# Two-layer graph network kernel: wider batches for gathering by rows, and a mask loaded for two groups at once

## The chip, the cores and the metric

The kernel runs on one core of one Trainium2 chip. Its metric is the device time of one execution in microseconds (us), lower being better. The median of three runs of the kernel before is 3950.51 us (3949.45 to 3950.6).

The engines are called PE (matrix products), DVE (vector), ACT (activations), POOL (GpSimd) and SP (Sync). SP, ACT and POOL each have a queue from which DMAs are issued, in the order of the program.

## The reference

The network has 12500 nodes with 128 features and 200000 edges that are sorted by destination. With `h = relu(layernorm(x))`:

```python
deg  = segment_sum(ones, dst, N);  wsum = segment_sum(edge_weight, dst, N)
w    = edge_weight / maximum(wsum, EPS)[dst]
feat = relu(h @ W_pool + b_pool)
neigh = segment_max(feat[src] * w[:, None], dst, N)          # layer 1
neigh = where(deg > 0, neigh, 0)
rst  = h @ W1_self + neigh @ W1_neigh + b1
h1   = relu(rst / maximum(norm(rst, axis=1), EPS))
neigh2 = segment_sum(h1[src] * w[:, None], dst, N) / maximum(deg, 1)   # layer 2
out  = x + relu(h1 @ W2_self + neigh2 @ W2_neigh + b2)
```

## The kernel before

**Stages.** A preparation normalises x, computes `feat` and writes it to `feat_d` in memory. Layer 1 then takes the edges in 391 groups of 512 (the last has 320), and writes its node results to `h_d`. Layer 2 takes the same 391 groups over `h_d` and writes the output. Each layer is one Python loop over "turns" `i`, which emits the instructions of several groups at different stages of their way (L638 for layer 1, L730 for layer 2). Each engine's instructions keep the order in which they are emitted.

**Gathers.** A group needs the source rows of its 512 edges: four chunks of 128 rows of 512 bytes. `gather` (L519) has POOL issue one indirect DMA for each chunk into the tile `gt` (L525), of which there are eight (L87), so that POOL can be at most eight groups ahead of the reader of `gt`.

**Chunks by rows.** In some groups chunk 0 does not come from POOL. The class `Rows` (L459) brings it into a tile `ga` by 128 DMAs of one row each, issued from SP's and ACT's queues. For group g, `load` (L494) has SP fetch the 128 source indices into a row `ri`, `shift` (L499) has DVE turn them into byte offsets, and `rows` (L502) loads a batch of offsets into registers of the issuing engine (a TENSOR_LOAD, L510) and issues one DMA for each (L514). The constructor's arguments say how often a group is taken (`every`) and how its rows are shared out: a list of (engine, rows, rows in a batch). `plan` spreads the batches of one chunk over the `every` turns that begin at turn g - every - 1. Before, layer 1 takes every 12th group (32 chunks), with 96 rows from SP in twelve batches of 8 and 32 rows from ACT in eight batches of 4 (L637). Layer 2 takes every 8th (48 chunks), with 64 rows from each queue in eight batches of 8 (L729). Groups 387 to 390 are never taken.

**A turn of layer 1.** SP issues its row batch (L640), stores a finished node tile if there is one (L576) and loads the mask `kt` of group i + 4 (L643). `kt` (L622 to L625) holds for each edge of a group whether its destination is that of the edge before, broadcast to all 128 partitions; seven tiles stand ready for it. POOL gathers group i. ACT scales the four chunks of group i by the edge weights (L654), waiting for the gathers and, in a taken group, for all rows of `ga`. PE transposes them into the tile `pm` (L655), of which there are two. DVE runs a segmented maximum over group i - 1 with `kt` (L661) and picks the results with two more operations (L669, L670), PE transposes these (L698) and puts them at their nodes' places (L710), and ACT writes the places of group i - 5 to `agg` (L703). Every fourth turn a tile of 128 nodes begins its own products (L552, L553). ACT's row batch stands at the turn's end (L713). Every second turn, some of the work on the edges' weights for later use goes to DVE as well.

**A turn of layer 2.** SP and ACT issue their row batches, POOL gathers group i, DVE builds a selection matrix of 192 columns, PE multiplies group i - 1 (L759) and DVE adds the sums of group i - 2 to `agg` (L764). A node tile's input is loaded and its output stored by SP every fourth turn (L585, L597).

**Semaphores of the DMAs.** In the built program, all DMAs of SP's and ACT's queues share eight semaphores, handed out in turn over both queues. A DMA waits until the one before it on its semaphore has landed. The order in which they are handed out is fixed when the program is built. In layer 1 it runs over turns that lie apart: SP's batch of a turn stands behind ACT's batches of turns some two to five later. POOL's gathers have eight semaphores of their own.

Of the kernel before, what the change touches and what calls it, by code (L numbers as in the profile page):

```python
# [8 lines left out]
BF16 = mybir.dt.bfloat16  # L9
# [9 lines left out]
P = 128  # L19
D = 128  # L20
G = 512
# [14 lines left out]
def gnn_kernel(ctx, tc, x, src, dst, ew, w_pool, b_pool, w1s, w1n, b1, w2s, w2n, b2, out):  # L36
# [13 lines left out]
    nc = tc.nc  # L50
# [6 lines left out]
    NG = GF + 1  # L57
# [7 lines left out]
    feat_d = dram.tile([NP, D], F32, name="feat_d")  # L65
    h_d = dram.tile([NP, D], F32, name="h_d")
    keep_d = dram.tile([NT * P, G], BF16, name="keep_d")
# [21 lines left out]
    wk = prep.enter_context(tc.tile_pool(name="n0", bufs=2))  # L89
# [293 lines left out]
    for i in range(len(groups) + 3):  # L383
        at = [groups[i - k] if 0 <= i - k < len(groups) else None for k in range(4)]
        if at[3]:
            t0, n = at[3]
# [7 lines left out]
        if at[2]:  # L394
            t0, n = at[2]
# [4 lines left out]
        if at[1]:  # L400
            t0, n = at[1]
# [11 lines left out]
        if at[0]:  # L413
            t0, n = at[0]
# [22 lines left out]
    def background():  # L437

        for t in range(1, NT):
            yield P * t - 4, edges1, t  # L440
        for t in range(NT):
            yield NG, edges2, t
        for t in reversed(range(NT)):
            yield NG, edges3, t
        for t in range(NT):
            yield NG, fitness, t
        yield NG, lambda get, t: verdict(get), 0

    def edges_of(g):

        ne = G if g < GF else TAIL
        return *divmod(g, P), ne, [(j, min(P, ne - j * P)) for j in range(-(-ne // P))]

    def pairs_of(g):

        t, r, ne, _ = edges_of(g)
        return t, r, ne, [(j, min(P, ne // 2 - j * P)) for j in range(-(-ne // (2 * P)))]
# [61 lines left out]
    def gather(pool, table_d, g, byrow=None):  # L519
        t, r, ne, chunks = edges_of(g)  # L520
        gt = pool.tile([P, Q, D], F32, name="gt")
        for j, k in chunks:
            if j == 0 and byrow and byrow.takes(g):
                continue
            nc.gpsimd.indirect_dma_start(  # L525
                out=gt[:k, j, :], out_offset=None, in_=table_d[:, :],
                in_offset=bass.IndirectOffsetOnAxis(ap=srcT[:k, t, j, r:r + 1], axis=0))
        return gt

    def turns(behind):  # L530

        out = {}
        g = i = 0
        for n in range(HI):
            while g < NG - 1 and (g + 1 - LAG) * RHO < (n + 1) * P:
                g += 1
            i = max(i + 1, g + behind)
            out[i] = n
        return out
# [64 lines left out]
    with tc.manual_schedule(), tc.tile_pool(name="ew", bufs=3) as wk, \  # L604
            tc.tile_pool(name="ep", bufs=2, space=PSUM) as ps:
        AHEAD = 4
        jobs = [(due, job(lambda: ps.tile([P, Q, P], F32, name="pq", bufs=1), t)) for due, job, t in background()]

        def side_step():

            while jobs:
                due, steps = jobs[0]
                if next(steps, jobs) is jobs:
                    jobs.pop(0)
                elif i < due:
                    break

        gts, kts, pms, scs, sels, prs, rws, pas = ({} for _ in range(8))
        turn = turns(6)
        busy = {}  # L620

        def keep_rows(g):  # L622
            ne = edges_of(g)[2]
            kts[g] = wk.tile([P, G], BF16, name="kt", bufs=AHEAD + 3)
            nc.sync.dma_start(kts[g][:, :ne], keep_d[g:g + 1, :ne].to_broadcast([P, ne]))  # L625

        def node_stage(k):
            if (i, k) in busy:
                st = busy.pop((i, k))
                next(st, None)  # L630
                if k < 5:
                    busy[i + 1, k + 1] = st

        for g in range(AHEAD):
            keep_rows(g)
        carry = NEG
        byrow = Rows(wk, feat_d, 12, [(nc.sync, 96, 8), (nc.scalar, 32, 4)])  # L637
        for i in range(max(turn) + 6):  # L638
            byrow.turn(i)
            byrow.rows(i, nc.sync)  # L640
            node_stage(5)
            if i + AHEAD < NG:
                keep_rows(i + AHEAD)  # L643
            if i < NG:
                gts[i] = gather(gp, feat_d, i, byrow)

            if i < NG:
                t, r, ne, chunks = edges_of(i)
                gs = wk.tile([P, Q, D], F32, name="gs", bufs=2)
                pms[i] = ps.tile([P, G], F32, name="pm")  # L650
                gt = gts.pop(i)
                for j, k in chunks:
                    rows_j = byrow.tile(i) if j == 0 and byrow.takes(i) else gt[:k, j, :]
                    nc.scalar.activation(gs[:k, j, :], rows_j, AF.Copy, scale=ewT[:k, t, j, r:r + 1])  # L654
                    nc.tensor.transpose(pms[i][:, j * P:j * P + k], gs[:k, j, :], ident[:k, :k])  # L655

            g = i - 1
            if 0 <= g < NG:
                ne = edges_of(g)[2]
                kt, pm = kts.pop(g), pms.pop(g)  # L660
                nc.vector.tensor_tensor_scan(pm[:, :ne], kt[:, :ne], pm[:, :ne], carry,  # L661
                                             op0=OP.add, op1=OP.max)
                if g + 1 < NG:
                    carry = wk.tile([P, 1], F32, name="carry")
                    nc.vector.tensor_copy(carry, pm[:, ne - 1:ne])
                sc = scs[g] = wk.tile([P, G // 2], F32, name="sc")
                two = pm[:, :ne].rearrange("p (c two) -> p c two", two=2)
                new = kt[:, :ne].bitcast(I16).rearrange("p (c two) -> p c two", two=2)
                nc.vector.tensor_copy(sc[:, :ne // 2], two[:, :, 1])  # L669
                nc.vector.copy_predicated(sc[:, :ne // 2], new[:, :, 1], two[:, :, 0])  # L670
            node_stage(1)
            node_stage(3)
            g = i - 3
            if 0 <= g < NG:
                t, r, ne, chunks = pairs_of(g)
                sels[g] = wk.tile([P, Q // 2, LW], F32, name="sel")
                for j, k in chunks:
                    nc.vector.tensor_scalar(  # L678
                        sels[g][:k, j, :], cols[:k, 1, :], lastT[:k, t, j, r:r + 1],
                        invT[:k, t, j, r:r + 1], op0=OP.is_equal, op1=OP.mult)  # L680

                rws[g] = wk.tile([P, Q // 2, D], F32, name="rows")
                pr = prs.pop(g)
                for j, k in (((slice(0, Q // 2), P),) if ne == G else chunks):
                    nc.scalar.activation(rws[g][:k, j, :], pr[:k, j, :], AF.Copy)  # L685

            node_stage(4)
            if i in turn:
                n = turn[i]
                st = nodes1(wk, ps, n, agg[:, n * P:(n + 1) * P])  # L690
                next(st)
                busy[i + 1, 1] = st
            g = i - 2
            if 0 <= g < NG:
                prs[g] = ps.tile([P, Q // 2, D], F32, name="pr")
                sc = scs.pop(g)
                for j, k in pairs_of(g)[3]:
                    nc.tensor.transpose(prs[g][:k, j, :], sc[:, j * P:j * P + k], ident)  # L698

            g = i - 5  # L700
            if 0 <= g < NG:
                at = window_at(mybir.EngineType.Activation, g)
                nc.scalar.activation(agg[:, bass.ds(at, LW)], pas.pop(g), AF.Copy)  # L703
            g = i - 4
            if 0 <= g < NG:
                chunks = pairs_of(g)[3]
                pas[g] = ps.tile([P, LW], F32, name="pa", bufs=1)
                rows, sel = rws.pop(g), sels.pop(g)
                for j, k in chunks:
                    nc.tensor.matmul(pas[g], rows[:k, j, :], sel[:k, j, :], start=j == 0,  # L710
                                     stop=j == len(chunks) - 1)
            node_stage(2)
            byrow.rows(i, nc.scalar)  # L713
            if i % 2:
                side_step()
        assert not busy
        i = NG
        side_step()


    with tc.manual_schedule(), tc.tile_pool(name="ew2", bufs=3) as wk, \
# [4 lines left out]
        gts, ss, pas, xrs = ({} for _ in range(4))  # L726
        turn = turns(3)
        late = None
        byrow = Rows(wk, h_d, 8, [(nc.sync, 64, 8), (nc.scalar, 64, 8)])  # L729
        for i in range(max(turn) + 2):  # L730
            byrow.turn(i)
            byrow.rows(i, nc.sync)
# [1 line left out]
            if i < NG:  # L734
                gts[i] = gather(gp, h_d, i, byrow)
                t, r, ne, chunks = edges_of(i)
# [11 lines left out]
            if i in turn:  # L748
                n = turn[i]
                late = nodes2(wk, ps, n, agg[:, n * P:(n + 1) * P], xrs.pop(n))  # L750
                next(late)
            g = i - 1
# [8 lines left out]
            g = i - 2  # L761
# [21 lines left out]
    with tc.If(flag > 0):  # L783
        with tc.tile_pool(name="gt", bufs=1) as tp, tc.tile_pool(name="gw", bufs=2) as wk, \
# [11 lines left out]
            for t0, n in node_groups():  # L796
                c = slice(t0 * P, (t0 + n) * P)
                k = n * P
# [87 lines left out]
```

## Time and profile before

| what | value |
|---|---|
| median of three runs | 3950.51 us |
| the profiled execution | 3949.8 us, of which its span 3947.9 us |
| POOL busy | 2946.2 us (75% of the span), 3105 instructions |
| PE busy | 2163.9 us (55%) |
| DVE busy | 1664.7 us (42%) |
| ACT busy | 795.0 us (20%) |
| first and last gather of layer 1 begin | 91.9 and 2023.9 us |
| first and last gather of layer 2 begin | 2045.8 and 3936.5 us |
| gathers of layer 1 and layer 2 | 1531 and 1515 |
| row DMAs of layer 1, SP and ACT | 3072 and 1024 |
| row DMAs of layer 2, SP and ACT | 3072 and 3072 |
| mask loads `kt` | 391, of 128 KB each (the last 80 KB) |

The page of a profile gives each engine's busy time, its groups of instructions (line, engine, operation, output and inputs, count, then busy time and mean, then the idle time just ahead of them and what ended most of it), and the waits. DMA-issuing instructions of SP and ACT are not counted as busy, and a DMA's arrival is not part of the issuing instruction's time. The indirect DMAs of POOL are counted[...].

### The profile page before, as it was taken

To read this page: it belongs to the slowest core of one execution; us is meant where nothing else is said; L and a number is where in the kernel's file an instruction comes from. 1 tells how busy PE (TensorE), PEld (TensorE's weight loads), DVE (VectorE), ACT (ScalarE), POOL (GpSimd) and SP (SyncE) were. 2 spreads that over 40 slices of the span, in tenths; PEclk is the share of its full clock that TensorE was granted. 3 is DMA by queue.
4 is the path that set the end of the run, shared out by engine and by line. 5 is a ranking of instruction groups with operands and counts; after the bars stand their busy time and mean duration, and the time that the engine had idled before them with its cause. 6 is when DMAs were issued, how large, how long until landed. Compare 5 with 4: busy or idle time off the path is not lost.

```text
span 3947.9 us, 55088 instructions
## 1 busy us (share of the span) xinstructions
PE 2163.9 (55%) x8349; PEld 1764.2 (45%) x8349; DVE 1664.7 (42%) x4700; ACT 795.0 (20%) x2907; POOL 2946.2 (75%) x3105
## 2 busy tenths in 40 slices
PE   6546546546555455445555555555555555555555
PEld 4335445435444344344444444444444444444444
DVE  7556656657656656556552222121221222222221
ACT  6334334334334334334320000000000000000000
POOL 5777777777777777777757777777777777777776
PEclk8555555555555555555555555555555555555555
DMA  6233333333333333333322222222222222222222
GB/s 170 75 83 85 84 84 84 84 83 82 84 84 82 85 85 84 85 86 83 86 65 61 62 63 61 62 62 62 62 62 62 62 62 62 62 62 62 62 62 58
DMA packets 245792, 295.43 MB, mean 75 GB/s; under 512 B 71023, under 2 KB 195518, under 8 KB 245424
## 3 DMA queue, kind: packets, MB, share of 16 engines
q0 software_dynamic: 97472, 199.75, 18.8%
q1 hardware_dynamic: 139024, 89.04, 8.4%
q10 hardware_dynamic: 8928, 3.03, 0.3%
q14 instruction: 296, 2.42, 0.2%
q8 instruction: 72, 1.18, 0.1%
HBM read 271.77 MB, written 19.77 MB: 74 GB/s over the span
## 4 chain that ended last, share of the span: by engine, by line
DMA 24%; POOL 23%; issue 17%; SPq 10%; PE 9%; DVE 7%; ACT 5%; ACTq 4%; POOLq 0%; DVEq 0%
POOL gt L525 23%; DMA gt<-h_d,srcT 14%; SPq L514 6%; PE pm L655 4%; DMA kt<-keep_d 4%; DVE pm L661 4%; DMA ga<-feat_d 3%; ACTq L514 3%; ACT gs L654 3%; SPq L510 2%; DMA ri<-in_src 1%; DMA gt<-feat_d,srcT 1%; PE pa L710 1%; SPq L625 1%; PE pn L552 1%
## 5 line engine op out<-in xcount | busy, mean ns | idle before, releaser
L525 POOL DMA_INDIRECT gt<-feat_d,srcT x1531 | 1466.1, 958 | 469.5 <-issue 391.4
L525 POOL DMA_INDIRECT gt<-h_d,srcT x1515 | 1429.5, 944 | 483.1 <-issue 388.3
L759 PE MATMUL pa<-s,gt 128*128 128x48 f32 x3030 | 967.9, 423 | 826.6 <-DMA gt<-h_d,srcT 736.1
L759 PEld LDWEIGHTS pa<-s,gt 128*128 128x128 f32 x3030 | 757.5, 312 | 1038.6 <-DMA gt<-h_d,srcT 818.6
L655 PE MATMUL pm<-ident,gs 128*128 128x128 f32 x1563 | 484.0, 439 | 902.0 <-DVE sc L670 497.3
L655 PEld LDWEIGHTS pm<-ident,gs 128*128 128x128 f32 x1563 | 288.5, 199 | 1038.2 <-issue 483.4
L764 DVE TENSOR_TENSOR agg<-pa,agg 128x48 f32 x391 | 81.2, 208 | 1439.3 <-PE pa L759 1025.7
L661 DVE TENSOR_TENSOR_SCAN pm<-kt,carry,pm 128x512 f32<-128x512 bf16 x390 | 499.3, 1280 | 255.1 <-DMA kt<-keep_d 118.2
L654 ACT ACTIVATE gs<-gt,ewT 128x128 f32<-128x128 f32 x1531 | 503.6, 392 | 357.0 <-DMA ga<-feat_d 200.6
L710 PEld LDWEIGHTS pa<-sel,rows 128*128 128x128 f32 x1564 | 352.5, 311 | 35.9 <-ACT agg L703 34.0
L710 PE MATMUL pa<-sel,rows 128*128 128x48 f32 x1564 | 358.0, 375 | 2.6 <-ACT agg L703 1.1
L698 PE MATMUL pr<-ident,sc 128*128 128x128 f32 x782 | 236.3, 403 | 0.8 <-DVE sc L670 0.7
L500 DVE TENSOR_SCALAR ri<-ri 1x128 int32<-1x128 int32 x80 | 18.2, 227 | 505.1 <-DMA ri<-in_src 495.7
L678 DVE TENSOR_SCALAR sel<-cols,lastT,invT 128x48 f32<-128x48 f32 x782 | 213.0, 327 | 0.0
L670 DVE COPY_PREDICATED sc<-kt,pm 128x256 f32<-128x256 int16 x391 | 173.0, 443 | 13.3
L698 PEld LDWEIGHTS pr<-ident,sc 128*128 128x128 f32 x782 | 163.0, 218 | 1.2 <-PE pa L710 1.0
L669 DVE COPY sc<-pm 128x256 f32<-128x256 f32 x391 | 162.0, 414 | 0.0
L741 DVE TENSOR_TENSOR s<-hit,w2T 128x192 f32<-128x192 f32 x391 | 139.8, 357 | 13.5
L685 ACT ACTIVATE rows<-pr 128x256 f32<-128x256 f32 x392 | 142.3, 363 | 2.2 <-PE pr L698 2.2
L739 DVE TENSOR_TENSOR hit<-iota,locT 128x192 f32<-128x192 f32 x391 | 139.1, 356 | 0.8
L703 ACT ACTIVATE agg<-pa 128x48 f32 x391 | 78.5, 201 | 162.4 <-PE pn L553 157.0
L565 ACT ACTIVATE sq<-r 128x128 f32<-128x128 f32 x98 | 29.7, 303 | 375.7 <-DVE r L561 375.7
(144 smaller groups left out, 1374.0 us busy)
## 6 DMA issues: line engine op xcount, KB each, us to landing
kt<-keep_d SPq DMA_DIRECT2D x390, 128.0 KB
ga<-feat_d SPq DMA_DIRECT2D x3072, 0.5 KB
ga<-h_d SPq DMA_DIRECT2D x3072, 0.5 KB
ga<-h_d ACTq DMA_DIRECT2D x3072, 0.5 KB
gt<-feat_d,srcT POOLq DMA_INDIRECT x1531
gt<-h_d,srcT POOLq DMA_INDIRECT x1515
ga<-feat_d ACTq DMA_DIRECT2D x1024, 0.5 KB
h_d<-h SPq DMA_DIRECT2D x98, 64.0 KB
```

What stands on the lines that cost most here:

```text
L514: eng.dma_start(ga[r + k:r + k + 1, :], self.bytes[None, bass.ds(at[k], 4 * D)])
L525: nc.gpsimd.indirect_dma_start(out=gt[:k, j, :], out_offset=None, in_=table_d[:, :], in_offset=bass.IndirectOffsetOnAxis(ap=srcT[:k, t, j, ...
L654: nc.scalar.activation(gs[:k, j, :], rows_j, AF.Copy, scale=ewT[:k, t, j, r:r + 1])
L655: nc.tensor.transpose(pms[i][:, j * P:j * P + k], gs[:k, j, :], ident[:k, :k])
L661: nc.vector.tensor_tensor_scan(pm[:, :ne], kt[:, :ne], pm[:, :ne], carry, op0=OP.add, op1=OP.max)
L669: nc.vector.tensor_copy(sc[:, :ne // 2], two[:, :, 1])
L670: nc.vector.copy_predicated(sc[:, :ne // 2], new[:, :, 1], two[:, :, 0])
L678: nc.vector.tensor_scalar(sels[g][:k, j, :], cols[:k, 1, :], lastT[:k, t, j, r:r + 1], invT[:k, t, j, r:r + 1], op0=OP.is_equal, op1=OP.mult)
L685: nc.scalar.activation(rws[g][:k, j, :], pr[:k, j, :], AF.Copy)
L698: nc.tensor.transpose(prs[g][:k, j, :], sc[:, j * P:j * P + k], ident)
L710: nc.tensor.matmul(pas[g], rows[:k, j, :], sel[:k, j, :], start=j == 0, stop=j == len(chunks) - 1)
L759: nc.tensor.matmul(pas[g], rows_j, s[:k, j, :], start=j == 0, stop=j == len(chunks) - 1)
```

## The change

Three things change. First, SP's batches of rows in layer 1 and both queues' batches in layer 2 become sixteen rows; ACT's in layer 1 stay at four. Second, layer 1 takes every 10th group instead of every 12th (38 chunks instead of 32), and layer 2 every 7th instead of every 8th (55 instead of 48). So 6 and 7 gathers go, and 13 times 128 row DMAs come. Third, `kt` is loaded for two groups at once, in odd turns: turn i loads groups i + 3 and i + 4. The number of its tiles falls from seven, of one group each, to the pool's own number, three (L604), of two groups each.

```diff
         def keep_rows(g):
-            ne = edges_of(g)[2]
-            kts[g] = wk.tile([P, G], BF16, name="kt", bufs=AHEAD + 3)
-            nc.sync.dma_start(kts[g][:, :ne], keep_d[g:g + 1, :ne].to_broadcast([P, ne]))
+
+            n = min(2, NG - g)
+            kt = wk.tile([P, 2, G], BF16, name="kt")
+            rows = keep_d[g:g + n, :]
+            nc.sync.dma_start(kt[:, :n, :], bass.AP(tensor=rows.tensor, offset=rows.offset,
+                                                    ap=[[0, P], [G, n], [1, G]]))
+            for k in range(n):
+                kts[g + k] = kt[:, k, :]
...
-        for g in range(AHEAD):
+        for g in range(0, AHEAD, 2):
             keep_rows(g)
         carry = NEG
-        byrow = Rows(wk, feat_d, 12, [(nc.sync, 96, 8), (nc.scalar, 32, 4)])
+        byrow = Rows(wk, feat_d, 10, [(nc.sync, 96, 16), (nc.scalar, 32, 4)])
         for i in range(max(turn) + 6):
             byrow.turn(i)
             byrow.rows(i, nc.sync)
             node_stage(5)
-            if i + AHEAD < NG:
-                keep_rows(i + AHEAD)
+            if i % 2 and i + AHEAD - 1 < NG:
+                keep_rows(i + AHEAD - 1)
...
-        byrow = Rows(wk, h_d, 8, [(nc.sync, 64, 8), (nc.scalar, 64, 8)])
+        byrow = Rows(wk, h_d, 7, [(nc.sync, 64, 16), (nc.scalar, 64, 16)])
```

The lines of `Rows`, `gather` and the loops are otherwise the same; from L626 on, the lines of layer 1 and layer 2 are numbered five higher.

## The prediction

> **What bounds the kernel now.** I read the groups of the page first, then POOL's timeline, then who waits on SP, DVE and ACT. In the groups, the last columns are busy time, mean ns, and the idle time ahead with what ended most of it:
>
> ```profile
> L525 POOL DMA_INDIRECT gt<-feat_d,srcT x1531 | 1466.1, 958 | 469.5 <-issue 391.4
> L525 POOL DMA_INDIRECT gt<-h_d,srcT x1515 | 1429.5, 944 | 483.1 <-issue 388.3
> ...
> L661 DVE TENSOR_TENSOR_SCAN pm<-kt,carry,pm 128x512 f32<-128x512 bf16 x390 | 499.3, 1280 | 255.1 <-DMA kt<-keep_d 118.2
> L654 ACT ACTIVATE gs<-gt,ewT 128x128 f32<-128x128 f32 x1531 | 503.6, 392 | 357.0 <-DMA ga<-feat_d 200.6
> ```
>
> POOL's timeline, far into layer 1 (start, duration, and in brackets the idle time before):
>
> ```profile
> 1600.41 0.94 POOL L525 DMA_INDIRECT gt<-feat_d,srcT  x1 [0.30 <-issue]
> 1601.66 0.95 POOL L525 DMA_INDIRECT gt<-feat_d,srcT  x1 [0.30 <-issue]
> 1602.91 0.95 POOL L525 DMA_INDIRECT gt<-feat_d,srcT  x1 [0.30 <-issue]
> ```
>
> A gather begins every 1.249 us, 0.945 of it busy and 0.305 between two. That holds throughout: layer 2's gathers begin from 2045.8 to 3936.5 us, 1890.7 us for 1514 steps, 1.2488 each. Layer 1's take 1932.0 us for 1530 steps, 1.2627; the trace puts the surplus of 21 us into 51 gathers of over 1.0 us, all before 1390 us, beside DVE's background work. POOL waits for no other engine, so it is the bound of both layers: a gather less is 1.2488 us less, as long as nothing else becomes late.
>
> What could become late is the chain by rows. SP's and DVE's longest waits in these stages, then the first use of the last chunk by rows in layer 1 beside POOL:
>
> ```profile
> SPq L514 <- DMA ga<-h_d: 301.4, 398, 5.4
> SPq L514 <- DMA ga<-feat_d: 257.8, 285, 5.4
> ```
>
> ```profile
> DVE ri L500 <- DMA ri<-in_src: 495.7, 35, 17.2
> DVE pm L661 <- DMA kt<-keep_d: 118.2, 64, 7.5
> ```
>
> ```profile
> 2012.62 0.94 POOL L525 DMA_INDIRECT gt<-feat_d,srcT  x1 [0.30 <-issue]
> 2012.80 0.40 ACT L654 ACTIVATE gs<-ga,ewT 128x128 f32<-128x128 f32 x1 [16.12 <-DMA ga<-feat_d]
> ```
>
> ACT starts group 384 at 2012.8 while POOL, counted back from its last gather, is at the second chunk of group 388. It would stop only at the start of group 392, where `gt` has no free tile, 15 gathers or 18.7 us on. In all 32 taken groups this lag (ACT's start less the end of the group's gathers) is 14 to 19 us, and ACT needs 8 to 11 turns to catch up. So layer 1's row chain is late in every cycle, and POOL is shielded from it by some 19 us.
>
> **What the Trainium skill says.** "Perfetto Trace Analysis", What "DMA-bound" means: an issuing queue whose track is solid DMA slices is bound by descriptor generation, not by data. POOL agrees (0.945 busy of 1.249). "DMA: Bandwidth & Descriptors", Anatomy of one DMA: about 2.0 us fixed plus bytes at 436 GB/s; the trace's gathers land 2.47 us and its `kt` loads of 128 KB 3.0 us after their issue begins. I take the difference for 128 KB more from it, an estimate of 0.3 us. The same page, Latency and other measured facts: a tensor_load takes about 600 ns at least. The trace shows 485 ns for most of ACT's loads of four registers, so the floor doesn't hold here; 742 ns is SP's median for eight:
>
> ```profile
> L510 SPq TENSOR_LOAD <-ri x768: 691/742/1054, 97.4 to 3884.8; - x192
> L510 ACTq TENSOR_LOAD <-ri x640: 312/823/1098, 98.9 to 3877.8; - x160
> ```
>
> **The change part by part.** *Gathers removed.* Multiples of 10 from 10 to 380 are 38, of 7 from 7 to 385 are 55, against 32 and 48. Layer 1 loses 6 x 1.2488 = 7.5 us, layer 2 7 x 1.2488 = 8.7 us: 16.2 us, if POOL stays fed.
>
> *Rows, layer 1, SP.* Its timeline where nothing waits:
>
> ```profile
> 1878.92 2.52 SPq L514 DMA_DIRECT2D ga<-feat_d  x8
> 1881.55 0.35 SPq L625 DMA_DIRECT2D kt<-keep_d  x1
> 1882.78 2.53 SPq L514 DMA_DIRECT2D ga<-feat_d  x8
> 1885.40 0.35 SPq L625 DMA_DIRECT2D kt<-keep_d  x1
> ```
>
> A turn is 3.86 us: eight rows at 0.323 = 2.58, a load of 0.72 and 0.13 around it, `kt` 0.43. Twelve turns are 46.3, three node stores of 0.42 and the `ri` load of 0.37 make 47.9 us per cycle. POOL takes 47 x 1.2488 = 58.7, so SP has 10.8 us to spare. After: a load of sixteen lies between 1.18 (0.058 us per register, from ACT's four to SP's eight) and 1.44 (no saving over two); I take 1.3. A batch is 16 x 0.323 + 1.3 + 0.13 = 6.6. Six are 39.6, five `kt` loads 2.2, 2.5 stores 1.05, `ri` 0.37: 43.2 us, against 39 x 1.2488 = 48.7 for POOL. The spare time falls from 10.8 to 5.5 us (4.6 to 6.2 by the load).
>
> *ACT, layer 1.* Eight batches of four per chunk stay, about 1.95 us each, now in 10 turns: 15.6 of 48.7 instead of 58.7 us. They stand between ACT's own operations, which need about 1.6 us a turn.
>
> *`kt`.* 195 issues of SP fewer at 0.43 us, counted above. A pair's first group is asked for one turn later than before (g - 3 instead of g - 4), and lands an estimated 3.3 us after issue instead of 3.0 (up to 4). The three tiles make SP wait for DVE's turn i - 1 instead of i - 2. Behind that wait stand the next row batch and the node store, and for these waits ACT. SP runs some five groups behind POOL, DVE at most four, so I price it at nothing (0 to 3 us of a cycle). DVE's wait on `kt` grows: 118 us now, hidden by the two `pm` tiles and by POOL's lead; without this cover, up to 3 us of a cycle.
>
> *The loop.* Spare time isn't all: SP waits for ACT through the shared semaphores, ACT for SP's last batch. The last batch now stands at turn g - 3 instead of g - 2. From the wait for ACT's rows three turns ahead to ACT's use of `ga`, the trace of before has 24 to 25.5 us of SP's work (1872.6 to 1896.7 in one cycle). After, three batches (19.6, its first load done earlier: 18.3), `kt`, a store, `ri` 1.3, landing 1.6: 21.2 to 22. ACT's part, from the use of one chunk to those rows, is 32 us before (1839.3 to 1871.3, 9 turns and six batches). After, 7 turns with six batches: two bare turns of 1.6 to 2.5 less, 27 to 29. Sum 48 to 51, against 48.7 for POOL (49.2 where its slow gathers fall): about level. A surplus of 0.5 us per cycle (19 us over 38 cycles) is still taken up by POOL's lead.
>
> *Layer 2.* Per 8 groups SP needs 8 x (0.78 + 0.15 + 2.58) = 28.1, 1.7 for stores and loads, 0.7 for `ri`: 30.5, plus some 3.4 of waits on semaphores; ACT's batches fill 33.4 of 38.7 us, and it then stands 5.75 us until the next offsets (3030.3 to 3036.1). After, 4 x (1.4 + 0.15 + 5.17) + 2.2 = 29.1, plus 3.4, 32.5 us, against 27 x 1.2488 = 33.7. A row lands 1.5 us after issue, so 133 DMAs on eight semaphores need 25 us. It fits, barely, and rows are complete about five groups ahead of use. Cost 0; without that cover, up to 1.3 us a cycle.
>
> *The rest.* DVE's background work is the same: its 21 us of slow gathers may shift by 4 either way. Between the layers POOL waits 21.9 us for the last nodes; the last chunk is now 380, not 384, so ACT may be 1 us earlier or, if it lags, later: 0. DMA traffic is no limit (84 GB/s).
>
> *Sum.* The profiled execution is 3949.8, 3947.9 of span and 1.9 around it. 3947.9 - 16.2 = 3931.7, with 1.9 it is 3933.6; the median is 0.7 above the profiled one, which makes 3934.
>
> **The rivals.** *A, POOL stays fed:* 3934, own range 3929 to 3938. For it: constant lag of 14 to 19 us in 32 cycles, 5.5 us of spare time on SP. Against it: the loop's sum. Chance 0.49.
> *B, layer 1's gain is eaten, layer 2's stays:* the loop is some 0.7 us a cycle over POOL: 38 x 0.7 = 27, less 19 of lead, 8 us lost: 3942 (3938 to 3948). Chance 0.14.
> *C, slower:* the row chain becomes layer 1's pace, at the taken group where ACT waits for `ga` (L659 after). The pair load's later first group adds a wait of DVE on `kt` ahead of a node's products, which hold ACT's rows, in about half the cycles: loop 50.9 instead of 49.2. 38 x 1.7 = 65, less 19 of lead, 46 us lost against 16 gained: 3980 (3958 to 4010). It decides from 0.5 us a cycle over POOL, and the total is slower from 0.9. For it: DVE's 118 us on `kt`, 496 us on `ri`. Layer 2 at 35 us a cycle would end similarly. Chance 0.37.
> That the change doesn't do what it says is ruled out by the built order: the loads, rows and gathers have the counts above.
>
> **How the numbers follow.** The likeliest case gives 3934. To hold 8 in 10, the range takes A and B (0.63) and C up to its middle: 3929 to 3980, leaving out half of C and the edge below. 0.2% is 7.9 us, about what a measurement of this kernel can tell from no change. Faster than 3942.6: A and half of B, 0.56. Within: the rest of B and the start of C, 0.09. Slower: 0.35.
>
> **What would show it.** Right: 1525 and 1508 gathers at 1.249 us with no wait of POOL on ACT or PE over 1 us; TENSOR_LOADs of 1.2 to 1.45 us; ACT's lag at taken groups level below 30 us; SP's waits on `ga` in layer 1 well below 258 us. Wrong: the lag grows cycle by cycle to 35 us and POOL then waits for L659; or, in layer 2, PE waits for `ga`.

## The result, and the profile after

The changed kernel takes 4084.22 us (4076.66 to 4090.12, 6 runs) against 3950.32 us for the kernel before (3948.66 to 3953.25, 6 runs). The ratio is 1.0338, 95% interval 1.0327 to 1.0349: slower by 3.4%, and above the predicted range. The profiled execution took 4076.66 us, 4074.9 of them its span.

In two of the later measurements the kernel before itself took 5840 and 5878 us, so no conclusion rests on what was measured beside it there.

The groups of the page after (busy time, mean ns, idle time ahead with what ended most of it):

```profile
L525 POOL DMA_INDIRECT gt<-feat_d,srcT x1525 | 1460.1, 957 | 600.0 <-issue 373.6
L525 POOL DMA_INDIRECT gt<-h_d,srcT x1508 | 1423.3, 944 | 489.9 <-issue 379.0
...
L666 DVE TENSOR_TENSOR_SCAN pm<-kt,carry,pm 128x512 f32<-128x512 bf16 x390 | 498.8, 1279 | 429.1 <-DMA kt<-keep_d 334.7
L659 ACT ACTIVATE gs<-gt,ewT 128x128 f32<-128x128 f32 x1525 | 489.0, 391 | 273.6 <-DMA ga<-feat_d 206.6
```

Busy times hardly differ. POOL's idle time ahead of layer 1's gathers rose from 469.5 to 600.0 us, and DVE's ahead of the scan from 255.1 to 429.1 us. In layer 2 POOL's idle time is as before.

| stretch, us | before | after | difference |
|---|---|---|---|
| start to first gather | 91.9 | 92.2 | +0.3 |
| first to last gather of layer 1 | 1932.0 | 2056.4 | +124.4 |
| to the first gather of layer 2 | 21.9 | 30.9 | +9.0 |
| first to last gather of layer 2 | 1890.7 | 1882.3 | -8.4 |
| to the end of the span | 11.4 | 13.1 | +1.7 |

The whole loss lies in layer 1 and just behind it. There, the gathers' steps exceed 1.2488 us by 153.2 us in all, against 21.3 before. POOL, which waited for no engine, now does. Below are POOL's timeline just after ACT has read the late chunk of group 300 (start, duration, idle time before), POOL's wait for ACT, and ACT's longest waits (total, times, longest):

```profile
1714.90 0.94 POOL L525 DMA_INDIRECT gt<-feat_d,srcT  x1 [4.55 <-ACT rows L690]
1716.14 0.94 POOL L525 DMA_INDIRECT gt<-feat_d,srcT  x1 [0.30 <-issue]
```

```profile
POOL gt L525 <- ACT rows L690: 144.9, 41, 6.3
```

```profile
ACT agg L708 <- PE pn L553: 416.3, 96, 15.4
ACT gs L659 <- DMA ga<-feat_d: 309.5, 180, 15.3
ACT sq L565 <- DVE r L561: 239.5, 29, 14.4
```

The name L690 only says that ACT was busy behind its late chunk: POOL waits for a tile of `gt` that ACT has yet to read. The sign that the prediction named for being wrong is there: ACT's lag at the taken groups is 13.0 us at group 10, 24.8 at 40, 36.8 at 70, and then stays at 37 to 40 until the last but one. From group to group ACT's first use of `ga` is 53.4 us apart (mean over the last two thirds of layer 1, the last cycle left out), and POOL would need 39 x 1.2488 = 48.7. 38 cycles of 4.7 us are 179; less the 25 us by which the lag grew, from 13 to 38, they come to about the 153 us above.

So the mechanism is that of rival C, layer 1 at the pace of its row chain, with a cycle of 53.4 us in place of C's 50.9. The question for the runs was what makes the cycle 53.4 us long.

**One cycle.** SP's timeline up to the last rows of group 300:

```profile
1689.38 12.19 SPq L514 DMA_DIRECT2D ga<-feat_d  x32
1701.67 0.36 SPq L627 DMA_DIRECT2D kt<-keep_d  x1
1702.13 0.24 SPq L497 DMA_DIRECT2D ri<-in_src  x1
1703.76 8.40 SPq L514 DMA_DIRECT2D ga<-feat_d  x16
...
1755.21 8.57 SPq L514 DMA_DIRECT2D ga<-feat_d  x16
```

(The last line is the same batch one cycle later.) DVE's timeline in the same stretch:

```profile
1704.24 0.22 DVE L500 TENSOR_SCALAR ri<-ri 1x128 int32<-1x128 int32 x1 [13.45 <-DMA ri<-in_src]
1704.49 1.29 DVE L666 TENSOR_TENSOR_SCAN pm<-kt,carry,pm 128x512 f32<-128x512 bf16 x1
...
1706.67 0.28 DVE L561 TENSOR_TENSOR r<-pn,b 128x128 f32<-128x128 f32 x1
```

And ACT's:

```profile
1706.99 0.31 ACT L565 ACTIVATE sq<-r 128x128 f32<-128x128 f32 x1 [13.93 <-DVE r L561]
...
1708.05 1.44 ACTq L514 DMA_DIRECT2D ga<-feat_d  x4
1713.35 0.40 ACT L659 ACTIVATE gs<-ga,ewT 128x128 f32<-128x128 f32 x1 [5.72 <-DVE sel L683]
...
1760.43 0.21 ACT L708 ACTIVATE agg<-pa 128x48 f32 x1 [13.82 <-PE pn L553]
```

Read in order of time: SP issues the indices `ri` of the next chunk only after 32 rows; DVE has waited for them for 13.45 us, and behind them stand a scan and the node's sum `r`; ACT has waited 13.93 us for `r`, and behind that stands its row batch; and SP's batch of sixteen, begun at 1703.76, lasts 8.40 us where sixteen rows need 16 x 0.323 = 5.2. The trace of its single rows shows why: the eighth begins at 1709.30, 3.45 us after the seventh, when ACT's row of 1708.05 has landed (1709.28) on the semaphore that both use. The Trainium skill, "Perfetto Trace Analysis", DMA Instruction — HWDGE, says that the profiler's start of such an instruction is when its semaphores are satisfied. This trace agrees: the rows' own records stay at 0.228 us or little more (0.268 at most in this batch), and the wait lies between two of them.

A cycle later it is the same, with ACT held at its copy to `agg` instead: L708 waits 13.82 us, ACT's row of 1760.90 lands at 1762.24, and the row of SP behind it begins at 1762.26.

It is a ring of three engines: SP's rows wait for ACT's, ACT's for DVE (at L708 by way of PE), DVE for what SP issues behind its rows. Nothing in it waits for POOL any more.

### The profile page after: what moved, and what is told of

The parts are those of the page before. It is cut to its first block, busy times and chain, and to the rows that moved or that the text cites. A ratio compares the mean times of both kernels' runs of the same rounds, so it can differ in the third digit from the quotient of the medians.

```text
span 4074.9 us, 57566 instructions
## 1 busy us (share of the span) xinstructions
PE 2069.8 (51%) x8349; PEld 1770.1 (43%) x8349; DVE 1655.9 (41%) x4713; ACT 795.9 (20%) x2907; POOL 2933.8 (72%) x3092
## 4 chain that ended last, share of the span: by engine, by line
DMA 37%; DVE 15%; SPq 15%; issue 9%; ACTq 9%; PE 7%; POOL 5%; ACT 3%; DVEq 0%; POOLq 0%
DMA ga<-h_d 22%; SPq L514 11%; DVE pm L666 6%; ACTq L514 5%; POOL gt L525 5%; DMA kt<-keep_d 5%; DMA ga<-feat_d 4%; ACTq L510 3%; DMA ri<-in_src 3%; SPq L510 3%; PE pm L660 3%; DMA gt<-h_d,srcT 2%; DVE sc L675 2%; DVE sc L674 2%; DVE sel L683 1%
## 5 line engine op out<-in xcount | busy, mean ns | idle before, releaser
L764 PE MATMUL pa<-s,gt 128*128 128x48 f32 x3016 | 850.4, 418 | 746.7 <-DMA gt<-h_d,srcT 451.3
L764 PEld LDWEIGHTS pa<-s,gt 128*128 128x128 f32 x3016 | 720.3, 320 | 875.5 <-DMA gt<-h_d,srcT 467.5
L660 PE MATMUL pm<-ident,gs 128*128 128x128 f32 x1563 | 466.5, 442 | 993.7 <-DVE sc L675 433.7
L666 DVE TENSOR_TENSOR_SCAN pm<-kt,carry,pm 128x512 f32<-128x512 bf16 x390 | 498.8, 1279 | 429.1 <-DMA kt<-keep_d 334.7
L659 ACT ACTIVATE gs<-gt,ewT 128x128 f32<-128x128 f32 x1525 | 489.0, 391 | 273.6 <-DMA ga<-feat_d 206.6
L715 PEld LDWEIGHTS pa<-sel,rows 128*128 128x128 f32 x1564 | 367.6, 323 | 34.2 <-ACT agg L708 33.1
L715 PE MATMUL pa<-sel,rows 128*128 128x48 f32 x1564 | 370.5, 385 | 1.1 <-ACT agg L708 0.7
L708 ACT ACTIVATE agg<-pa 128x48 f32 x391 | 78.4, 201 | 425.5 <-PE pn L553 416.3
L690 ACT ACTIVATE rows<-pr 128x256 f32<-128x256 f32 x392 | 142.9, 365 | 88.8 <-PE pr L703 88.8
L553 PE MATMUL pn<-w_2n,agg 128*128 128x128 f32 x196 | 64.3, 432 | 85.5 <-DVE agg L769 85.5
```

The lines of the kernel that those rows point to most:

```text
L764: nc.tensor.matmul(pas[g], rows_j, s[:k, j, :], start=j == 0, stop=j == len(chunks) - 1)
```

## The experiments

Lengths of a cycle in what follows are worked out as above, from ACT's first uses of `ga` over the last two thirds of layer 1, the last cycle left out. POOL's own need is 58.7 us at every 12th and 48.7 at every 10th group, and a little more where its slow gathers fall.

| kernel | time, us | ratio, 95% interval | cycle, us |
|---|---|---|---|
| before | 3950.32 | | 59.3 |
| after | 4084.22 | 1.0338 (1.0327 to 1.0349) | 53.4 |
| `kt` in pairs only | 3953.95 | 1.0006 (0.9999 to 1.0013) | 59.3 |
| layer 2 only | 3943.46 | 0.9980 (0.9970 to 0.9989) | |
| layer 1, batch 16 only | 4015.91 | 1.0164 (1.0147 to 1.0181) | 61.4 |
| after, `kt` single | 4153.19 | 1.0511 (1.0493 to 1.0528) | 55.1 |
| after, batch 8 in layer 1 | 4081.60 | 1.0326 (1.0309 to 1.0343) | 53.4 |
| after, `ri` early | 4158.70 | 1.0524 (1.0507 to 1.0542) | 55.4 |
| layer 1, batch 16, `ri` early | 4020.40 | 1.0174 (1.0157 to 1.0191) | 61.5 |
| after, ACT's rows first | 3936.64 | 0.9962 (0.9948 to 0.9977) | 49.2 |
| after, ACT's rows in the middle | 3950.25 | 1.0004 (0.9996 to 1.0013) | 49.8 |
| after, ACT's rows first, batch 8 | 3939.70 | 0.9980 (0.9969 to 0.9991) | 49.6 |

Each ratio is against runs of the kernel before that were measured beside it (3951.85, 3951.57, 3949.43 and 3949.76 us for the experiments).

### The parts, one by one

My theory was first that the ring closes too slowly only at every 10th group. Its rivals: the pairs of `kt`, or the sixteens.

`kt` in pairs alone: the function of the diff, and the other two edits left out.

> The kernel before with only the masks kt loaded for two groups at once into three tiles; rows as before (every 12th and 8th group, batches of 8). Loop theory (layer 1 is paced by the loop of SP's rows, ACT's rows and DVE's shift of the indices, which closes too slowly only at every 10th group): no change, 3946 to 3955 us, DVE's wait on kt somewhat above 118 us. Pair theory (the later masks alone hold DVE, and through it ACT's rows): the loop of before has about 1 us to spare in 58.7 and gets up to 3 us more, so 32 x 2 us less 19 us of lead, about 3990 us.

3953.95 us, no change. DVE's wait on `kt` grew more than expected, from 118 to 386 us, and its wait on `ri` shrank from 496 to 276: these two waits together rose by only 49 us, and ACT's lag at the taken groups stayed at 12 to 20 us. The pairs alone cost nothing that the runs can tell.

The reverse, the kernel after with `kt` as before:

```diff
-            kt = wk.tile([P, 2, G], BF16, name="kt")
...
+            kts[g] = wk.tile([P, G], BF16, name="kt", bufs=AHEAD + 3)
```

> The kernel after with kt as before: one group per load, seven tiles. Loop theory: still late, 4040 to 4080 us; SP issues five loads more per cycle (2.2 us), and DVE loses part of its waits on kt. Pair theory: the loss is gone, 3930 to 3945 us, with POOL at 1.249 us per gather throughout.

4153.19 us, worse than either said. The pair theory is out: pairs save 69 us here. The cycle is 1.7 us longer, and the five more issues of `kt`, at 0.43 us each, are 2.2 us: most of what SP has to do more seems to count in the ring.

Layer 2 alone, `Rows(wk, h_d, 7, ...)` with batches of sixteen:

> The kernel before with only layer 2 changed: every 7th group in batches of sixteen. Seven gathers fewer at 1.2488 us, no stall of POOL in layer 2: 3941 to 3943 us by every theory that puts the whole loss into layer 1. If batches of sixteen hurt layer 2 as well, 3950 or more.

3943.46 us against 3951.85: 8.4 us faster for seven gathers, 8.7 by the sum, which lies within the interval (0.9970 to 0.9989, or 4 to 12 us). Layer 2 does what was forecast.

The sixteens alone:

```diff
-        byrow = Rows(wk, feat_d, 12, [(nc.sync, 96, 8), (nc.scalar, 32, 4)])
+        byrow = Rows(wk, feat_d, 12, [(nc.sync, 96, 16), (nc.scalar, 32, 4)])
```

> The kernel before with only SP's batches in layer 1 raised from 8 to 16 rows; every 12th group and kt as before. Loop theory: six batches in twelve turns leave SP more spare time (about 43 of 58.7 us), so no change, 3946 to 3955 us. Batch theory (sixteen rows in one piece hold back the masks, the indices and so DVE): POOL stalls on ACT in layer 1 and the time is 3970 us or more.

4015.91 us: my theory missed this. With the same chunks and less work for SP the ring takes 61.4 us and passes POOL's 58.7. SP's and ACT's timelines of that kernel in one cycle:

```profile
1738.52 0.83 SPq L625 DMA_DIRECT2D kt<-keep_d  x2
1740.68 10.13 SPq L514 DMA_DIRECT2D ga<-feat_d  x16
1750.91 0.35 SPq L625 DMA_DIRECT2D kt<-keep_d  x1
```

```profile
1746.60 0.21 ACT L703 ACTIVATE agg<-pa 128x48 f32 x1 [7.36 <-PE pn L553]
1747.23 1.44 ACTq L514 DMA_DIRECT2D ga<-feat_d  x4
```

Sixteen rows last 10.13 us, held by ACT's rows of 1747.23, and these by the copy to `agg`, which waited 7.36 us for PE (PE itself had waited for DVE). Meanwhile the next masks stand behind the sixteen rows; DVE's wait on `kt` is 254 us, from 118. By this cycle it is the same ring, entered by a longer batch. A rival stands beside this reading. With sixteens, a row of SP that follows one of ACT's on its semaphore follows one of 2.5 turns later on average, by the traces; in the kernel before it was 1.9 turns (0 to 4, and not the two to five that the description of that kernel has). No run changed the batch and kept that order.

The kernel after, with layer 1's batches back at eight rows:

> The kernel after with SP's batches in layer 1 back at 8 rows (12 batches in 10 turns, 44.8 us of SP per cycle without waits); every 10th group and kt in pairs stay. Batch theory (sixteen rows in one piece hold back masks and indices): most of the loss goes, 3935 to 3965 us. Density theory (38 chunks are too many for the loop, whatever the batch): 4050 us or more.

4081.60 us, as after: at every 10th group, the ring is too slow with either batch. Eight rows cost SP 2.0 us a cycle more in loads (twelve of 0.781 us in place of six of 1.228), and its waits on `ga` in layer 1 are less by (322 - 195) / 38 = 3.3 us. So each of the two edits to layer 1's rows is enough for a loss (1.6% and 3.3%), and going back to batches of eight alone doesn't help.

### Which link to cut

The first candidate was the load of `ri`. Here SP issues it five turns earlier, in layer 1 (`early` is 5 there, and nothing in layer 2):

```diff
-            for g, lead, step in ((i + self.every + 2, -1, self.shift), (i + self.every + 3, -2, self.load)):
+            for g, lead, step in ((i + self.every + 2, -1, self.shift), (i + self.every + 3 + self.early, -2, self.load)):
```

> The kernel after, but in layer 1 SP loads a chunk's source indices five turns earlier; DVE's shift stays where it is. Link theory (SP's load of the indices holds DVE's shift, DVE holds a node's products, ACT's rows stand behind these, and SP's last batch waits for them: some 3.2 to 5 us of the 53.3 us per cycle): DVE's wait on ri falls from 1146 us to below 300, and the time to 3940 to 3990 us. If only the rows' length or the shared semaphores count: still 4060 or more.

4158.70 us, worse. DVE's two waits in that kernel, over both layers:

```profile
DVE pm L666 <- DMA kt<-keep_d: 841.5, 150, 14.6
DVE ri L500 <- DMA ri<-in_src: 645.2, 48, 20.5
```

Up to the end of layer 1 alone the wait on `ri` fell from 427.5 us in the kernel after to 6.4 (what is left is layer 2's, where nothing was moved), and the wait on `kt`, which is all layer 1's, rose from 335 to 842. SP issues both behind its rows, so with one link gone the ring closes through the other. Why it is worse rather than equal isn't settled. The moved load also shifts how semaphores are handed out: where a row of SP follows one of ACT on a semaphore, that is by the traces a row of 2.9 turns later on average, in place of 2.5. No run separates this.

The same edit on the kernel with only the sixteens:

> The kernel before with SP's batches in layer 1 at 16 rows (4016 us with that alone), and its source indices loaded five turns earlier. Link theory: a cycle falls from 61.0 us by about 3.7, below POOL's 58.7, so 3945 to 3960 us. If the batch's length itself is the cause: 4005 us or more.

4020.40 us, no gain, and the same picture: DVE's wait on `ri` 467 to 40 us, on `kt` 254 to 607. The theory that `ri` is the decisive link falls twice.

The other place to cut is between DVE and ACT's rows. Here ACT's row batch stands in each turn right behind the scaling of the group, ahead of everything that waits for DVE's recent results:

```diff
                     nc.tensor.transpose(pms[i][:, j * P:j * P + k], gs[:k, j, :], ident[:k, :k])
+            byrow.rows(i, nc.scalar)
...
             node_stage(2)
-            byrow.rows(i, nc.scalar)
```

> The kernel after with ACT's row batch moved, in each turn, ahead of ACT's operations that wait for DVE and PE (it then stands right after the scaling of the group). Link theory: ACT's rows are held less by DVE, SP's waits on ga fall from 322 us, 3950 to 4040 us. If ACT's place in the turn doesn't matter: 4070 to 4095 us.

3936.64 us: the loss is gone, more fully than I expected, and the kernel beats both others. Its groups for POOL, and ACT's first use of one chunk:

```profile
L525 POOL DMA_INDIRECT gt<-feat_d,srcT x1525 | 1463.3, 960 | 467.7 <-issue 364.0
L525 POOL DMA_INDIRECT gt<-h_d,srcT x1508 | 1424.9, 945 | 477.6 <-issue 383.3
```

```profile
1596.91 0.40 ACT L659 ACTIVATE gs<-ga,ewT 128x128 f32<-128x128 f32 x1 [4.69 <-DMA ga<-feat_d]
```

POOL's idle time in layer 1 is 467.7 us, as before the change, with six gathers fewer; ACT's lag stays at 12 to 17 us in all 38 cycles, and SP's waits on `ga` in layer 1 fall from 322 to 149 us. In layer 1 DVE still waits 261 us for `kt` and 384 for `ri`: here these waits cost nothing, so in the kernel after it wasn't these waits as such that cost the time, but what stood behind them on ACT. The distance on the semaphores is 2.6 turns here, 2.5 in the kernel after, so a shorter distance on them isn't what helped.

Which of the operations ahead of the rows mattered? Here the batch stands behind ACT's copy of the picked rows (L690), but ahead of its copy to `agg` (L708) and of a node's square (L565):

```diff
                     nc.scalar.activation(rws[g][:k, j, :], pr[:k, j, :], AF.Copy)
+            byrow.rows(i, nc.scalar)
```

> The kernel after with ACT's row batch between ACT's copy of the picked rows (L690) and its copy to agg (L708), taken a third time because the kernel before took 5840 and 5878 us in the calls of the first two. Place theory, if the waits that hold ACT's rows are those of L708 and L565 (416 and 240 us in the kernel after): nearly all of the loss goes, 3935 to 3960 us. If it is L690's (89 us): 4040 us or more.

3950.25 us. Passing L708 and L565 brings back 134 us, passing L690 too the last 14. The waits at L708 and a node's square held the rows (a node's copy L580 was passed as well; its longest wait in the kernel after is 2.2 us). What L690 adds makes the ring 49.8 us, just over POOL, and the lag creeps up from 11 to 36 us through the layer.

Last, are the sixteens needed once the place is right?

> The kernel after with ACT's rows first and SP's batches in layer 1 at 8 rows, taken a third time because the kernel before took 5840 and 5878 us in the calls of the first two. Place theory: SP needs 44.8 us of a cycle of 48.7 without waits, and the waits of the run with ACT's rows first were 3.9 us a cycle: just at POOL's pace, 3936 to 3955 us. If batches of sixteen are what made that run good: 3990 us or more.

3939.70 us, 0.9969 to 0.9991: faster than before too, with the lag rising from 15 to 30 us. So the sixteens give the ring a little room (49.2 us against 49.6); the 3 us between the totals are not clear of noise, since the two intervals overlap.

### Four kernels beside 5840 and 5878 us

Four kernels were measured twice beside a kernel before of 5840 and 5878 us: ACT's rows in the middle, the kernel before with ACT's rows first, ACT's rows first with batches of eight, and ACT's rows first with every 9th group. The first time:

> The kernel after with ACT's row batch between ACT's copy of the picked rows (L690) and its copy to agg (L708): behind the former, ahead of the latter and of a node's square (L565). Place theory, if the waits that hold ACT's rows are those of L708 and L565 (416 and 240 us in the kernel after): nearly all of the loss goes, 3935 to 3960 us. If it is L690's (89 us), whose rows come from DVE two turns back: 4040 us or more.

> The kernel before with ACT's row batch right after the scaling of the group, nothing else. POOL paces both layers there, so by the place theory no change: 3946 to 3955 us, with SP's waits on ga in layer 1 below 258 us. If the place itself saves work: faster than 3940 us.

> The kernel after with ACT's rows first and SP's batches in layer 1 at 8 rows. Place theory: SP needs 44.8 us of a cycle of 48.7 without waits, and the waits of the run with ACT's rows first were 149 us in 38 cycles, 3.9 each: 48.7, just at POOL's pace, so 3936 to 3955 us. If batches of sixteen are what made that run good: 3990 us or more.

> The kernel after with ACT's rows first and every 9th group in layer 1 (42 chunks, four gathers fewer). SP then needs about 42.9 us of POOL's 43.7 per cycle, and some 3 to 4 us of waits on top: SP becomes the pace of layer 1, 42 x 3 us less 19 us of lead, about 4040 us (3970 to 4080). If POOL stays fed after all: 3936.6 - 4 x 1.2488, 3931.6 us.

Beside 5840 us for the kernel before they took 6098, 5715, 6152 and 6203 us. The second time:

> The kernel after with ACT's row batch between ACT's copy of the picked rows (L690) and its copy to agg (L708); taken again, since the kernel before took 5840 us in the call of the first try. Place theory, if the waits that hold ACT's rows are those of L708 and L565 (416 and 240 us in the kernel after): nearly all of the loss goes, 3935 to 3960 us. If it is L690's (89 us): 4040 us or more.

> The kernel before with ACT's row batch right after the scaling of the group, nothing else; taken again for the same reason. Place theory: POOL paces both layers, so no change, 3946 to 3955 us, with SP's waits on ga in layer 1 below 258 us. If the place itself saves work: faster than 3940 us.

> The kernel after with ACT's rows first and SP's batches in layer 1 at 8 rows; taken again for the same reason. Place theory: SP needs 44.8 us of a cycle of 48.7 without waits, and the waits of the run with ACT's rows first were 3.9 us a cycle: just at POOL's pace, 3936 to 3955 us. If batches of sixteen are what made that run good: 3990 us or more.

> The kernel after with ACT's rows first and every 9th group in layer 1 (42 chunks, four gathers fewer); taken again for the same reason. SP needs about 42.9 us of POOL's 43.7 per cycle and some 3 to 4 us of waits on top: 42 x 3 us less 19 us of lead, about 4040 us (3970 to 4080). If POOL stays fed after all: 3936.6 - 4 x 1.2488, 3931.6 us.

Beside 5878 us: 6125, 5741, 6180 and 6225 us. None of these expectations is decided by such numbers. The first and the third kernel have times beside a kernel before of 3949 to 3950 us too, 3950.25 and 3939.70 us, as told above. The second and the fourth have none: whether the place alone changes the kernel before at its usual speed, and where the row chain ends next, stays open. A fourth tile for pairs of masks, which would let SP load them two turns earlier, wasn't tried.

## Why the prediction was wrong, step by step

- *Gathers removed, 16.2 us*: right. Layer 2's stretch fell by 8.4 of 8.7 us, and with ACT's rows first the total fell by 14.9 us.
- *Layer 2 at no cost*: right; POOL has no step over 1.4 us there.
- *A load of sixteen, 1.3 us; a batch, 6.6 us*: right. The profile's rows for the loads of both layers:

```profile
L510 ACTq TENSOR_LOAD <-ri x524: 315/487/1488, 98.9 to 4017.0; - x175
L510 SPq TENSOR_LOAD <-ri x448: 1133/1229/1432, 95.4 to 4024.2; - x150
```

  1.229 us, so a batch is 6.5.
- *SP has 5.5 us to spare in layer 1*: true as work, and no protection. SP's waits there:

```profile
SPq L514 <- DMA ga<-feat_d: 321.6, 291, 8.3
...
SPq L514 <- DMA kt<-keep_d: 45.5, 88, 1.7
```

  They are 9.7 us for each of 38 cycles, and 43.2 of work with 9.7 of waits are 52.9, the measured 53.4 within half a us.
- *`kt` in pairs at nothing*: right as a change by itself, shown by its own run; and in the slow ring it saves 1.7 us a cycle. A pair landed 3.31 us after its issue began (median of those that DVE waited for in the kernel after; 3.02 for a single load before), as the estimate of 3.3 had it. The fit that this estimate was taken from is given by the Trainium skill, "DMA: Bandwidth & Descriptors", Anatomy of one DMA, for POOL's DMAs and not for SP's; here it served for SP's all the same.
- *The loop, 48 to 51 us*: this step failed. It was 52.9 us in the cycle above (1660.42 to 1713.35) and 51.9 in the next. ACT's part came out as forecast or better: from ACT's use at 1660.42 to its rows at 1687.81 are 27.4 us (27 to 29 forecast), in the next cycle 25.1 (to 1738.42). SP's part was forecast as 21.2 to 22 us and took 24.0 (1689.38 to 1713.35) and 24.7 in the next (1740.50 to 1765.21). Two terms were missing. The sum took every batch at the pace of its rows and had only one wait of SP for ACT in a cycle; there is a second one, inside the last batch: 8.40 and 8.57 us where 5.2 were counted, behind ACT's rows, DVE and the indices that SP itself had issued just ahead. And between the two parts ACT's row has to land before SP goes on, which stood in neither: 1.6 us from 1687.81 to 1689.38. (In the next cycle SP was busy with the batch before and its load until 1740.50, 2.1 us.) In rival C I had a second wait, but at 1.7 us, in half the cycles and put down to the mask; it came in both of these cycles, once through L565 and once through L708, at 3.2 to 3.4 us.

  Both terms stood in the very cycle of the kernel before that the sum was taken from, counted there as SP's work or not at all. ACT's row of 1871.27 had to land before SP went on at 1872.60, and the last batch of that chunk waited behind ACT as well (SP's line, then ACT's two):

```profile
1891.39 3.95 SPq L514 DMA_DIRECT2D ga<-feat_d  x8
```

```profile
1890.60 0.31 ACT L565 ACTIVATE sq<-r 128x128 f32<-128x128 f32 x1 [12.77 <-DVE r L561]
...
1891.66 1.44 ACTq L514 DMA_DIRECT2D ga<-feat_d  x4
```

  Eight rows need 2.6 us and took 3.95.
- *The choice of A*: its main argument, the steady lag of 14 to 19 us in the kernel before, showed only that POOL was then the slower of the two. DVE's 496 us on `ri` and 118 on `kt` and ACT's waits behind DVE were in the profile before; I read them as idle time of engines that aren't the bound, and did not ask, beyond what C had, what stood behind them on the next engine.
- *When C decides*: it fits, far from the limit. The total was to be slower from 0.9 us a cycle over POOL; it was 4.7 over. The lead that POOL could lose first was larger than the 19 us counted on, about 25 (a lag of 13 to 38).

The cause, as far as it is shown: ACT's row batch stood behind operations that wait for DVE, which closed a ring of SP, DVE and ACT; moving that batch alone removes the loss. That the ring runs through the shared semaphores is read from the built program and from single rows of SP that begin when ACT's row on the same semaphore has landed; no run gave the queues semaphores of their own. The Trainium skill, "Trainium Architecture — The Big Picture", Inside one NeuronCore, says that a core has 256 semaphores and that engines synchronize only through them. No run here shows that number: in these programs the two queues share eight.

## What to carry to other kernels

When queues share semaphores, look at what stands ahead of each DMA-issuing instruction on its own engine: move the issue ahead of operations that wait for other engines before adding DMAs to it. Here an engine's spare time and a steady lag didn't tell how long a ring of engines takes to close; add up the ring once with every wait and landing in it, and count each place where one engine's issue stands behind another's result. If a ring is suspected, cutting one feed may only pass the wait to the next one, as it did here, so look for the place where all of them meet.

## What the runs showed of the hardware

A TENSOR_LOAD of sixteen registers takes 1.229 us on SP and 1.300 on ACT (median, layer 2), after 0.718 to 0.782 and 0.828 for eight and 0.484 for four on ACT: about 0.06 us for each register more from eight to sixteen (on ACT 0.09 from four to eight), so sixteen in one load save some 0.25 us on SP and 0.36 on ACT against two of eight. Where the kernel before took 5840 and 5878 us, stretches of SP's queue ran at about 0.70 us, or twice that, from one instruction to the next, also for register moves that otherwise take 0.029 us, and so did some of ACT's; POOL and DVE show no more such steps there than in the kernel before at 3950 us. The kernels with more chunks by rows lost most: 6098 to 6225 us, against 5715 to 5878 for those with the chunks of before. What set that off isn't known.
